# Products of row pairs on VectorE: per-row multiplies taken out, a larger share for ScalarE

## The chip, the cores and the metric

The kernel runs on one core of a Trainium2 chip. The metric is the device time of one execution in microseconds (us), from outside the kernel. A core has several engines with an instruction stream each. Three matter here: VectorE (DVE in the profile), ScalarE (ACT) and SyncE (SP), which here does nothing but issue DMA transfers. A transfer between the on-chip memory and HBM is split over 16 DMA engines, and it has landed when the last of them is done with its part.

## The reference

The input is a matrix of 4096 rows with 256 fp32 numbers each. For every row the kernel computes all products x[i]·x[j] with i ≤ j, in the order of the upper triangle: first the 256 products with i = 0, then 255 with i = 1, and so on to the single one with i = 255.

```python
dot = jnp.einsum('bi,bj->bij', inputs, inputs)
iu, ju = jnp.triu_indices(256)
return dot[:, iu, ju]          # (4096, 32896) fp32
```

The output has 4096 × 32896 × 4 bytes, 539 MB, from an input of 4.19 MB.

## The kernel before, in words

**Tiling.** The 4096 rows lie on 128 partitions, 32 rows to a partition. The whole input is loaded once into the tile x, by three DMAs (L124). Then the kernel walks over 16 groups (`g`); a group is REPEAT = 2 rows on every partition. In each group the 32896 output columns are cut into five pieces (`c`) of 6528 or 6592 columns. A piece of a group is one output tile o of 128 × 2 × 6592 numbers, 52 KB per partition, from a pool of three buffers (`opool`, bufs=3), and leaves by one DMA (L164). Only the very first piece leaves in four parts, cut at the columns in FIRST. So there are 16 × 5 + 3 = 83 output DMAs, all on SP's queue, in program order.

**Product rows.** A "product row" is a run of columns with one i: the number x[i] of a row times the stretch x[i..255] of the same row. `runs` lists the product rows of a piece as (i, j, at, n): first factor, first column of the second, place in the output, length n. Long rows come first: piece 0 has rows of 256 down to 231 products, piece 4 has rows of 114 down to 1. At a border of a piece a row is cut in two.

**Who computes what.** `split` gives the first (longest) product rows of a piece to ScalarE, as few as leave VectorE within a budget: BUDGET × REPEAT × columns, in nanoseconds by the kernel's own estimates (`vector_time`). ScalarE makes a product row with one ACTIVATE for each of the two repeats (L137), the number x[i] being the scale. With the budget of 1.08 ScalarE has no row of piece 0 in groups 1 to 15, and 2, 3, 4 and 15 rows of the pieces 1 to 4. In the very first piece the budget is 0: there the rows are halved between the engines by estimated time.

**VectorE's three ways.** `vector_ops` chooses among: "each", one tensor_scalar (L149) for each repeat of a row, x[i] as a per-partition scalar; "two", one tensor_tensor (L158) for two neighbouring rows and both repeats, where x[i] and x[i+1] are read with a step of 0; "all", one tensor_tensor for one row and both repeats. "Each" is chosen where the estimate REPEAT·(130 + 0.52·n) is not above that of the tensor_tensor. That is so for rows of some 215 products and more: all of piece 0, and about half of the columns of piece 1.

**Order.** `interleave` alternates between the first and the second half of a piece's operations, so that neighbouring instructions write far apart. Which engine waits for what is set by the framework: an engine's first instruction on a piece waits until the DMA that last emptied this buffer has landed; the DMA of a piece waits for both engines that wrote it.

Of the kernel before, what the change touches and what calls it, by code (L numbers as in the profile page):

```python
# [1 line left out]

# [4 lines left out]

F32 = mybir.dt.float32
AF = mybir.ActivationFunctionType
ALU = mybir.AluOpType  # L10

P = 128
UNIT = 64
REPEAT = 2
PIECES = 5
BUDGET = 1.08
FIRST = [512, 1536, 3584]


def even_borders(lo: int, hi: int, pieces: int) -> list[int]:  # L20
    units = (hi - lo) // UNIT
    return [lo + units * c // pieces * UNIT for c in range(pieces)] + [hi]


def runs(d: int, lo: int, hi: int) -> list:


    found, at = [], 0
    for i in range(d):
        a, b = max(at, lo), min(at + d - i, hi)  # L30
        if a < b:
            found.append((i, i + a - at, a, b - a))
        at += d - i
    return found


def vector_ops(block: list) -> list:

    ops, k = [], 0
    while k < len(block):
        i, j, at, n = block[k]
        two = k + 2 < len(block) and i == j
        each = REPEAT * (130 + 0.52 * n)
        together = 68 + 1.046 * REPEAT * n - (34 if two else 0)
        if each <= together:
            ops.append(("each", block[k]))  # L50
        elif two:
            ops.append(("two", block[k]))
            k += 1
        else:
            ops.append(("all", block[k]))
        k += 1
    return ops


def interleave(block: list) -> list:  # L60


    half = len(block)
    while half and len(vector_ops(block[:half])) > len(vector_ops(block[half:])):
        half -= 1
    a, b = vector_ops(block[:half]), vector_ops(block[half:])
    return [op for k in range(max(len(a), len(b))) for ops in (a, b) for op in ops[k : k + 1]]


def vector_time(block: list) -> float:  # L70
    t = 0.0
    for way, (i, j, at, n) in vector_ops(block):
        if way == "each":
            t += REPEAT * (130 + 0.52 * n)
        else:
            t += 68 + 1.046 * REPEAT * n * (2 if way == "two" else 1)
    return t


def split(block: list, budget: float) -> int:  # L80


    scalar, k = 0.0, 0
    while k < len(block):
        scalar += REPEAT * (184 + 0.837 * block[k][3])
        if vector_time(block[k:]) <= budget or scalar > vector_time(block[k + 1 :]):
            break
        k += 1
    return k


def window(ap: bass.AP, free: list) -> bass.AP:
    return bass.AP(ap.tensor, ap.offset, [list(ap.ap[0]), *free])


@with_exitstack
def kernel(
    ctx: ExitStack, tc: tile.TileContext, x: bass.AP, out: bass.AP
):

    nc = tc.nc
    n, d = x.shape
    width = out.shape[1]
    assert n % (P * REPEAT) == 0 and width == d * (d + 1) // 2 and width % UNIT == 0
    groups = n // (P * REPEAT)
    borders = even_borders(0, width, PIECES)
    slot = max(b - a for a, b in zip(borders, borders[1:]))  # L110

    xpool = ctx.enter_context(tc.tile_pool(name="x", bufs=1))
    opool = ctx.enter_context(tc.tile_pool(name="o", bufs=3))

    x_in = x.rearrange("(p r) d -> p (r d)", p=P)
    x_out = out.rearrange("(p g r) c -> g p r c", p=P, r=REPEAT)


    total = n // P * d
    xt = xpool.tile([P, total + 1], F32, name="x")  # L120
    nc.vector.memset(xt[:, total:], 0.0)  # L121
    cuts = [0, REPEAT * d, total // 2, total]
    for a, b in zip(cuts, cuts[1:]):
        nc.sync.dma_start(xt[:, a:b], x_in[:, a:b])  # L124

    for g in range(groups):
        for c, (lo, hi) in enumerate(zip(borders, borders[1:])):
            o = opool.tile([P, REPEAT, slot], F32, tag="o", name=f"o_{g}_{c}")
            first = g == c == 0
            cuts = [lo, *(FIRST if first else []), hi]  # L130
            for a, b in zip(cuts, cuts[1:]):
                block = runs(d, a, b)
                k = split(block, 0.0 if first else BUDGET * REPEAT * (b - a))
                for i, j, at, length in block[:k]:
                    for r in range(REPEAT):
                        row = (g * REPEAT + r) * d
                        nc.scalar.activation(  # L137
                            o[:, r, at - lo : at - lo + length],
                            xt[:, row + j : row + j + length],
                            AF.Copy,  # L140
                            scale=xt[:, row + i : row + i + 1],
                        )
                row = g * REPEAT * d
                for way, (i, j, at, length) in interleave(block[k:]):
                    at -= lo
                    if way == "each":
                        for r in range(REPEAT):
                            row_r = row + r * d
                            nc.vector.tensor_scalar(  # L149
                                o[:, r, at : at + length],  # L150
                                xt[:, row_r + j : row_r + j + length],
                                xt[:, row_r + i : row_r + i + 1],
                                None,
                                ALU.mult,
                            )
                        continue
                    m = 2 if way == "two" else 1
                    nc.vector.tensor_tensor(  # L158
                        o[:, :, at : at + m * length],
                        window(xt[:, row + j :], [[d, REPEAT], [1, m], [1, length]]),  # L160
                        window(xt[:, row + i :], [[d, REPEAT], [1, m], [0, length]]),
                        ALU.mult,
                    )
                nc.sync.dma_start(x_out[g][:, :, a:b], o[:, :, a - lo : b - lo])  # L164


# [1 line left out]
_INS = ["r_inputs"]  # L168
_OUTS = [((4096, 32896), "float32")]


# [20 lines left out]
```

## Time and profile before

| | before |
|---|---|
| time, median of 7 runs | 1277.84 us (1277.73 to 1278.0) |
| the profiled execution: its own time | 1277.79 us |
| span from first to last instruction in it | 1276.0 us |
| so outside the span | 1.79 us |
| VectorE busy | 1129.2 us, 2978 instructions |
| of these tensor_tensor (L158) | 805.7 us, 1651 |
| of these tensor_scalar (L149) | 346.1 us, 1326 |
| ScalarE busy | 234.7 us, 787 instructions |
| DMA over the span | 426 GB/s mean |

How to read it: busy time is the time in which an engine executed something, and idle time of an engine that is not the bottleneck costs nothing. The GB/s are what all 16 DMA engines moved together. The share of the DMA engines can be a little above 1 in short windows, since packets are counted whole.

### The profile page before, as it was taken

How to read it: one execution, taken by the hardware profiler on the slowest of the kernel's cores; microseconds unless marked ns; L12 is line 12 of the kernel's file. 1: busy time of each engine (PE TensorE's matmuls, PEld its weight loads, DVE VectorE, ACT ScalarE, POOL GpSimd, SP SyncE). 2: the span in 40 equal slices, each digit the busy share in tenths (PEclk: the TensorE clock that was granted, in tenths of full speed). 3: DMA queues.
4: the chain of work that ended last, by engine and by line, in shares of the span. 5: the costliest groups of instructions: out<-in, count | busy, mean ns of one | idle time of the engine just before them, and what ended most of it. 6: DMA issues, size and time to landing. Idle time of an engine off the chain costs nothing.

```text
span 1276.0 us, 4106 instructions
## 1 busy us (share of the span) xinstructions
DVE 1129.2 (88%) x2978; ACT 234.7 (18%) x787; POOL 0.2 (0%) x4
## 2 busy tenths in 40 slices
DVE  8999989898898988989889898898988989888880
ACT  4211112121121301213012130121301213012130
POOL 0000000000000000000000000000000000000000
DMA  9999999999999999999999999999999999999997
GB/s 387 431 435 428 430 431 426 433 424 434 430 430 429 430 431 426 435 423 434 425 433 429 429 434 425 433 425 434 428 430 432 427 433 425 433 425 434 428 430 314
DMA packets 23040, 543.43 MB, mean 426 GB/s; under 512 B 1376, under 2 KB 1376, under 8 KB 2016
## 3 DMA queue, kind: packets, MB, share of 16 engines
q1 hardware_dynamic: 23008, 543.17, 99.5%
q14 instruction: 32, 0.26, 0.0%
HBM read 4.19 MB, written 538.97 MB: 426 GB/s over the span
## 4 chain that ended last, share of the span: by engine, by line
DMA 62%; DVE 35%; issue 0%; DVEq 0%; SPq 0%
DMA out_dram<-o 62%; DVE o L158 24%; DVE o L149 11%; DMA x<-in_r_inputs_dram 0%; SPq L164 0%; DVEq L158 0%; DVEq L149 0%; DVEq L188 0%
## 5 line engine op out<-in xcount | busy, mean ns | idle before, releaser
L158 DVE TENSOR_TENSOR o<-x 128x104 f32<-128x104 f32 (+60 forms) x1651 | 805.7, 570 | 59.1 <-DMA out_dram<-o 59.1
L137 ACT ACTIVATE o<-x 128x197 f32<-128x197 f32 (+25 forms) x786 | 233.4, 384 | 1000.5 <-DMA out_dram<-o 918.8
L149 DVE TENSOR_SCALAR o<-x 128x216 f32<-128x216 f32 (+5 forms) x1326 | 346.1, 342 | 52.9 <-DMA out_dram<-o 50.2
L137 ACT ACT_TABLE_LOAD x1 | 1.3, 1283 | 0.7 <-PEq L179 0.7
L121 DVE MEMSET x<- 128x1 f32 x1 | 0.1, 59 | 0.8 <-PEq L179 0.8
L179 POOL MEMSET const-bfloat16-1.0<- 128x1 bf16 x1 | 0.1, 102 | 0.0
L179 POOL MEMSET const-uint8-127<- 128x1 uint8 x1 | 0.1, 101 | 0.0
L179 POOL MEMSET const-float32-0.0<- 128x1 f32 x1 | 0.1, 99 | 0.2 <-issue 0.2
L179 POOL MEMSET const-float32-1.0<- 128x1 f32 x1 | 0.1, 98 | 0.0
## 6 DMA issues: line engine op xcount, KB each, us to landing
out_dram<-o SPq DMA_DIRECT2D x64, 6592.0 KB, 32.9
out_dram<-o SPq DMA_DIRECT2D x15, 6528.0 KB, 33.3
out_dram<-o SPq DMA_DIRECT2D x1, 2944.0 KB, 16.7
x<-in_r_inputs_dram SPq DMA_DIRECT2D x1, 2048.0 KB, 12.5
out_dram<-o SPq DMA_DIRECT2D x1, 2048.0 KB, 13.7
x<-in_r_inputs_dram SPq DMA_DIRECT2D x1, 1792.0 KB, 7.1
out_dram<-o SPq DMA_DIRECT2D x1, 1024.0 KB, 11.7
out_dram<-o SPq DMA_DIRECT2D x1, 512.0 KB, 10.6
```

The source lines that it names most:

```text
L121: nc.vector.memset(xt[:, total:], 0.0)
L137: nc.scalar.activation(o[:, r, at - lo : at - lo + length], xt[:, row + j : row + j + length], AF.Copy, scale=xt[:, row + i : row + i + 1],)
L149: nc.vector.tensor_scalar(o[:, r, at : at + length], xt[:, row_r + j : row_r + j + length], xt[:, row_r + i : row_r + i + 1], None, ALU.mult,)
L158: nc.vector.tensor_tensor(o[:, :, at : at + m * length], window(xt[:, row + j :], [[d, REPEAT], [1, m], [1, length]]), window(xt[:, row + ...
L179: nc = _bacc.Bacc("TRN2", target_bir_lowering=False, num_devices=1)
```

## The change

VectorE loses the way "each": it makes pairs of rows by one tensor_tensor, and a row that has no partner by a tensor_tensor of its own. The budget goes from 1.08 to 0.95, so that `split` gives ScalarE more of the first rows of each piece. Loads, pieces, buffers, output DMAs and the order of the pieces stay.

```diff
-BUDGET = 1.08
+BUDGET = 0.95
...
     ops, k = [], 0
     while k < len(block):
         i, j, at, n = block[k]
-        two = k + 2 < len(block) and i == j
-        each = REPEAT * (130 + 0.52 * n)
-        together = 68 + 1.046 * REPEAT * n - (34 if two else 0)
-        if each <= together:
-            ops.append(("each", block[k]))
-        elif two:
-            ops.append(("two", block[k]))
-            k += 1
-        else:
-            ops.append(("all", block[k]))
-        k += 1
+        m = 2 if k + 2 < len(block) and i == j else 1
+        ops.append((block[k], m))
+        k += m
     return ops
...
 def vector_time(block: list) -> float:
-    t = 0.0
-    for way, (i, j, at, n) in vector_ops(block):
-        if way == "each":
-            t += REPEAT * (130 + 0.52 * n)
-        else:
-            t += 68 + 1.046 * REPEAT * n * (2 if way == "two" else 1)
-    return t
+    return sum(68 + 1.046 * REPEAT * n * m for (*_, n), m in vector_ops(block))
...
-                for way, (i, j, at, length) in interleave(block[k:]):
+                for (i, j, at, length), m in interleave(block[k:]):
                     at -= lo
-                    if way == "each":
-                        for r in range(REPEAT):
-                            row_r = row + r * d
-                            nc.vector.tensor_scalar(
-                                o[:, r, at : at + length],
-                                xt[:, row_r + j : row_r + j + length],
-                                xt[:, row_r + i : row_r + i + 1],
-                                None,
-                                ALU.mult,
-                            )
-                        continue
-                    m = 2 if way == "two" else 1
                     nc.vector.tensor_tensor(
```

What that makes of the two streams, counted in the instruction order of the built programs (an ACTIVATE on ScalarE is one row of one repeat):

| piece, groups 1 to 15 | ScalarE rows before → after | VectorE instructions before → after |
|---|---|---|
| 0 | 0 → 4 | 54 → 13 |
| 1 | 2 → 6 | 38 → 14 |
| 2 | 3 → 7 | 19 → 17 |
| 3 | 4 → 9 | 24 → 21 |
| 4 | 15 → 22 | 52 → 48 |

In the very first piece ScalarE keeps its nine rows, and VectorE's 39 instructions become 17. Over the whole program VectorE goes from 2978 to 1813 instructions and ScalarE from 787 to 1547, without those that only wait.

## The prediction

> **What bounds the kernel now.** I read the page first: busy shares, DMA slices, queues, issues.
>
> ```profile
> span 1276.0 us, 4106 instructions
> ...
> DVE 1129.2 (88%) x2978; ACT 234.7 (18%) x787; POOL 0.2 (0%) x4
> ...
> DMA  9999999999999999999999999999999999999997
> ...
> q1 hardware_dynamic: 23008, 543.17, 99.5%
> q14 instruction: 32, 0.26, 0.0%
> ...
> out_dram<-o SPq DMA_DIRECT2D x64, 6592.0 KB, 32.9
> ```
>
> The DMA engines are full in every slice but the last. A piece lands 32.9 us after its issue, and 6592 KB (6.75 MB) at the 430 GB/s of the middle slices take 15.7 us: two pieces are always queued, so VectorE, with 14.2 us of work in a piece, is early. The chain of waits gives it 35%, but only because the chain runs back through buffers; VectorE itself waits for landings (59.1 + 50.2 us). So the end is set by bytes. What is left is that a transfer ends with its *slowest* DMA engine. I looked at the busy time in windows at the end, when the last piece drains (columns: window, length, busy DVE, ACT, POOL, clock, DMA share, GB/s).
>
> ```profile
> 1266.00:1267.00 1.00, 0.00 (x0) 0.00 (x0) 0.00 (x0) 1.00 0.98 422
> 1267.00:1268.00 1.00, 0.00 (x0) 0.00 (x0) 0.00 (x0) 1.00 0.25 106
> 1268.00:1269.00 1.00, 0.00 (x0) 0.00 (x0) 0.00 (x0) 1.00 0.12 53
> 1269.00:1270.00 1.00, 0.00 (x0) 0.00 (x0) 0.00 (x0) 1.00 0.06 26
> ...
> 1273.00:1274.00 1.00, 0.00 (x0) 0.00 (x0) 0.00 (x0) 1.00 0.06 26
> 1274.00:1275.00 1.00, 0.00 (x0) 0.00 (x0) 0.00 (x0) 1.00 0.00 0
> ```
>
> A share of 0.06 is one engine of sixteen, 0.12 two. Most engines end at about 1267.2, a second-last one at about 1269, and one works alone until 1274: **6.8 us in which one DMA engine decides.** What has it done that the others have not? The page's last DMA row names the only other traffic: 32 packets of "instruction", 128 of the program's 4106 instructions in each. In a window of 1 us (286 to 287) one such packet takes 1.9% of 16 engines, 0.30 us. VectorE's 2978 instructions are 2978/128 = 23.3 packets, times 0.30 us 7.0 us, against 6.8 on the last engine; ScalarE's 787 are 6.1 packets, 1.8 us, against 1.8 on the second-last. I conclude that each engine's instructions come over one DMA engine, which so falls behind. The landings agree. ScalarE or VectorE starts a piece when a buffer's transfer has landed:
>
> ```profile
> 566.20 2.00 ACT L137 ACTIVATE o<-x 128x75 f32<-128x75 f32 x6 [14.26 <-DMA out_dram<-o]
> 581.56 2.63 ACT L137 ACTIVATE o<-x 128x143 f32<-128x143 f32 x8 [13.36 <-issue]
> 597.16 8.24 ACT L137 ACTIVATE o<-x 128x37 f32<-128x37 f32 x30 [12.97 <-DMA out_dram<-o]
> ```
>
> ```profile
> 613.50 13.86 DVE L149 TENSOR_SCALAR o<-x 128x256 f32<-128x256 f32 x54 [2.00 <-DMA out_dram<-o]
> 629.09 3.52 DVE L149 TENSOR_SCALAR o<-x 128x228 f32<-128x228 f32 x14 [1.73 <-DMA out_dram<-o]
> ```
>
> The steps are 15.36, 15.60, 16.34, 15.59 us. An instruction packet lies in the third stretch and in none of the others; the next stretch with a long step, 629.09 to 645.41 (16.32 us), has one again.
>
> **The change part by part.**
>
> *Instructions.* VectorE has 1165 fewer (2978 to 1813): 9.1 packets. At 0.30 us each its DMA engine falls behind by 2.7 us less: 6.8 − 2.7 = 4.1 us behind the rest. ScalarE has 760 more (787 to 1547), 5.9 packets: 1.8 + 1.8 = 3.6 us behind, so VectorE's stays the last, by 0.5 us. Gain **2.7 us**. Bounds for a packet: nothing from below (if the late engine is late for another reason), and from above the 0.75 us by which a landing with a packet comes later than one without (16.3 against 15.5); 9.1 × 0.75 = 6.8 would close the whole gap. I take 0.30: the tail adds up all 23 packets (6.8/23.3 = 0.29), while a landing shows a packet's first effect, part of which is caught up (15.36 is shorter than 15.6).
>
> The Trainium skill speaks against any effect: "Runtime: NRT & Kernel Launch", section "Instruction fetch mechanics", has instructions refilled in 16 KiB blocks of 256 by a queue of the sequencer's own, at a cost that is mostly hidden. It is hidden from the engine, as the trace agrees; but 32 packets of 8 KB (0.26 MB) are what the page has, and the tail shows where they go. By the rule the sum would be 0 and the time 1277.8 us.
>
> *VectorE's work.* A tensor_scalar takes 350 ns at 128x256, the tensor_tensor of 128x856 1046 and that of 128x400 580 ns (rows by shape). Start to start it is less: the chain has 0.96 us for a 128x856 and 0.49 us for two tensor_scalars of 224. From 856 and 400 elements a tensor_tensor costs (1046 − 580)/456 = 1.02 ns per element, and about 0.08 us on top start to start. Piece 0 keeps 5510 of its 6528 columns (rows 256 to 253 go): 13 instructions, 2 × 5510 × 1.02 ns + 13 × 0.08 = 12.3 us, against 13.86 now. Pieces 1 to 4 come to 12.2, 12.3, 12.3 and 12.8 us alike (5424, 5344, 5189, 4371 columns and 14, 17, 21, 48 instructions), from 14.2 to 14.4 now. All are under the 15.7 us of a transfer, with 31 us in the queue: **0 us**. Without that cover, if VectorE bound, the 1.5 to 2 us of a piece times 80 would be 120 us or more; nothing of it counts here.
>
> *ScalarE's work.* 30 activations of piece 4 take 8.24 us (row at 597.16), 0.275 each; 44 make 12.1 us. In the other pieces 8 to 18 activations, at the 0.47 us of the 128x229 row, are at most 8.5 us, all under 15.7: **0 us**. If ScalarE bound, the transfers would start late by what exceeds 31 us; it is far from that. In piece 0 ScalarE now waits for the buffer's landing, and the DMA for ScalarE too. Queued behind that wait is only its work on later pieces, whose buffers come free later still; and 3.3 us of ScalarE end long before VectorE's 12.3.
>
> *The start.* The queue fills from the loads on, so late first work could open a gap. The fourth DMA of the first piece is issued when VectorE ends that piece, at 13.2 us (in the chain 30 tensor_scalars follow from 9.29 us on in 7.40 us, the first 16 of them this piece's). Its 17 tensor_tensors take 0.6 to 0.8 us longer (9 ScalarE rows unchanged). The parts land 10.6, 11.7, 13.7 and 16.7 us after issue, for 1.2 to 7.0 us of bytes each: over 8 us of queue lie ahead of every one. The tightest is piece 1, issued at 27.5 us, with 18.1 us to landing (the issues of 27 to 28 us) for 15.7 us of bytes: 2.4 us of margin. It gains: 0.7 us later start, 1.9 us less work. **0 us.**
>
> *The queue.* SP issues the same three loads and 83 outputs, with the same sizes, in the same order: 0 us.
>
> Sum against the profiled execution: 1277.79 − 2.7 = **1275.1 us**, of which 1.79 lie outside the span as before. The median, 1277.84, stands 0.05 above it.
>
> **The rivals.**
>
> *Nothing moves* (1277.8 us): the late engine is late for something else, or ScalarE's packets, up from 6 to 12, load the same engine and take back 1.8 of 2.7 (1276.9). For it: no view says which engine a packet uses. Against it: two products, 7.0 and 1.8 us, fit two tails, 6.8 and 1.8.
>
> *The whole gap closes* (1271.0): with packets further apart each delay is caught up, at 0.75 us for each of the 9.1. Against it: in 23 packets not more than 0.29 us each was left over, so little is open to be caught up.
>
> *ScalarE's extra traffic slows the output* (slower than before). 760 activations more are busy for some 250 us (233.4 us now; the rows above add up to some 475). Windows of piece 4 with ScalarE busy and after it:
>
> ```profile
> 754.80:763.00 8.20, 8.20 (x25) 8.20 (x30) 0.00 (x0) 1.00 0.98 419
> 763.00:771.00 8.00, 6.13 (x28) 0.04 (x1) 0.00 (x0) 1.00 0.99 422
> ...
> 912.50:920.60 8.10, 8.10 (x25) 8.10 (x30) 0.00 (x0) 1.00 1.00 427
> 920.60:928.60 8.00, 6.17 (x28) 0.08 (x1) 0.00 (x0) 1.00 1.00 425
> ```
>
> 419 and 427 against 422 and 425: no sign, to within 1%. At 1.1% over 250 us (2.7 us) the gain is gone; from 2.1% on (5.3 us) the kernel is measurably slower; 3% gives 1275.1 + 7.5 = 1282.6 us.
>
> **How the numbers follow.** Forecast 0.62, nothing moves 0.20, whole gap 0.10, slower 0.08. The forecast's own spread is ±1 us (one packet more or less, at up to 0.75 us, and the second-last engine 0.5 us behind). The range takes the forecast, nearly all of "nothing moves" and the upper half of the way to the whole gap: 1273.3 to 1278.1; the ends left out are 1271 and 1283. A measurement of this kernel tells about 0.2% from no change, 2.56 us, so the line is at 1275.28, and the forecast at 1275.1 stands just beyond it: some 0.6 of its 0.62 falls there. Faster 0.37 + 0.10 = 0.47; same 0.25 + 0.20 = 0.45; slower 0.08.
>
> **What would show it.** Right: some 29 instruction packets instead of 32 on the page; most DMA engines end within 1 us of 1267.2, and the single engine's tail is some 4 us instead of 6.8, with a second one close to it; landings of 16.3 us come less often; VectorE is busy for about 990 us, ScalarE for about 480, and both wait longer for landings. Wrong: a tail of 6.8 us or more with fewer instructions; GB/s of the middle slices below 425; SP waiting with an empty queue; a landing less than 31 us after its issue in the middle.

## The result, and the profile after

| | before | after |
|---|---|---|
| median | 1277.90 us (34 runs, 1277.73 to 1278.05) | 1274.63 us (14 runs, 1273.79 to 1274.93) |
| the profiled execution | 1277.79 us, span 1276.0 | 1274.85 us, span 1273.1 |

The ratio of after to before is 0.9974, 95% interval 0.9967 to 0.9980: faster by 0.26%, 3.3 us. The profiled executions differ by 2.94 us. The page of the changed kernel, the lines that answer to those shown of before:

```profile
span 1273.1 us, 3732 instructions
...
DVE 996.1 (78%) x1813; ACT 486.7 (38%) x1547; POOL 0.2 (0%) x4
...
q14 instruction: 29, 0.24, 0.0%
...
out_dram<-o SPq DMA_DIRECT2D x64, 6592.0 KB, 34.8
```

VectorE is busy for 133 us less and ScalarE for 252 us more, and neither shows in the time: the queue is as full as it was (34.8 us from issue to landing). What has changed is in the instruction row, 29 packets instead of 32, and in the way the last piece drains (the busy time in windows at the end, columns as before):

```profile
1265.00:1266.00 1.00, 0.00 (x0) 0.00 (x0) 0.00 (x0) 1.00 1.17 501
1266.00:1267.00 1.00, 0.00 (x0) 0.00 (x0) 0.00 (x0) 1.00 0.43 185
1267.00:1268.00 1.00, 0.00 (x0) 0.00 (x0) 0.00 (x0) 1.00 0.13 53
...
1269.00:1270.00 1.00, 0.00 (x0) 0.00 (x0) 0.00 (x0) 1.00 0.12 53
1270.00:1271.00 1.00, 0.00 (x0) 0.00 (x0) 0.00 (x0) 1.00 0.06 26
1271.00:1272.00 1.00, 0.00 (x0) 0.00 (x0) 0.00 (x0) 1.00 0.00 0
```

Two DMA engines (0.12) now work on for some 4 us, one of them a little longer. Before, one worked alone until 1274. The last engine is earlier by 3 us, and ScalarE's has come close behind it.

The trace also has the 16 landing marks of each transfer, one for each DMA engine. They size the tail better than windows of 1 us, so the table has for every run of this study how far the last and the second-last part of the last transfer land behind the median part, and when that median part lands, from the span's start. The instructions are those of the built programs.

| run | VectorE / ScalarE instructions | packets on the page | last / second part behind the median, us | median part lands | time, median us |
|---|---|---|---|---|---|
| before | 2980 / 789 | 32 | 7.50 / 2.76 | 1267.6 | 1277.90 |
| after | 1815 / 1549 | 29 | 4.81 / 3.92 | 1267.3 | 1274.63 |
| e1 | 2935 / 1549 | 38 | 10.00 / 4.06 | 1267.7 | 1280.57 |
| e2 (GpSimd 1128) | 1815 / 1549 | 38 | 4.53 / 4.01 | 1267.7 | 1274.96 |
| e3 | 2618 / 1519 | 35 | 6.05 / 3.72 | 1266.8 | 1275.60 |
| e4 | 2006 / 851 | 24 | 4.56 / 1.94 | 1268.2 | 1275.53 |
| e5 | 2921 / 1549 | 37 | 6.78 / 4.13 | 1267.5 | 1277.37 |
| e6 | 3393 / 1549 | 41 | 9.77 / 3.88 | 1267.6 | 1280.05 |
| e7 | 1078 / 875 | 17 | 2.27 / 1.80 | 1283.2 | 1288.43 |
| e8 | 1014 / 1415 | 22 | 3.36 / 2.73 | 1282.2 | 1288.32 |
| e9 | 3238 / 2089 | 45 | 13.25 / 11.86 | 1261.8 | 1278.07 |
| e10 | 1719 / 1835 | 30 | 2.96 / 2.79 | 1265.7 | 1271.45 |

Of the 2.94 us between the two profiled executions, 2.69 are the last part's lag (7.50 to 4.81), and 0.26 are the median part, which lands earlier.

Landing by landing the marks also show whose packets delay which part. An instruction packet comes when VectorE's stream (instructions that only wait counted) stands 49 to 76 instructions past a multiple of 128, or ScalarE's 54 to 82; one packet in each of the two runs is SyncE's. In the kernel before, from the fourth piece on, the lag of the last part rises at 23 landings, by 0.6 to 0.8 us, and falls at all others, by some 0.15 us; each of the 23 follows a VectorE packet. In the changed kernel there are 14 such landings, with 0.7 to 1.0 us. Where a ScalarE packet comes alone before the change (at 271, 650, 840 and 1044 us), the second-last part rises, by 0.6 to 0.8 us, and the last one falls.

### The profile page after: what moved, and what is told of

Its sections match the earlier page's. It is cut to its first block, busy times and chain, and to the rows that moved or that the text cites. A ratio compares the mean times of both kernels' runs of the same rounds, so it can differ in the third digit from the quotient of the medians.

```text
span 1273.1 us, 3732 instructions
## 1 busy us (share of the span) xinstructions
DVE 996.1 (78%) x1813; ACT 486.7 (38%) x1547; POOL 0.2 (0%) x4
## 4 chain that ended last, share of the span: by engine, by line
DMA 68%; DVE 29%; issue 0%; SPq 0%; DVEq 0%
DMA out_dram<-o 67%; DVE o L132 29%; DMA x<-in_r_inputs_dram 1%; DVEq L132 0%; SPq L138 0%; SPq L110 0%
## 5 line engine op out<-in xcount | busy, mean ns | idle before, releaser
L132 DVE TENSOR_TENSOR o<-x 128x356 f32<-128x356 f32 (+61 forms) x1812 | 996.1, 634 | 240.3 <-DMA out_dram<-o 237.3
L123 ACT ACTIVATE o<-x 128x253 f32<-128x253 f32 (+41 forms) x1546 | 485.4, 404 | 749.1 <-DMA out_dram<-o 747.5
## 6 DMA issues: line engine op xcount, KB each, us to landing
out_dram<-o SPq DMA_DIRECT2D x64, 6592.0 KB, 34.8
x<-in_r_inputs_dram SPq DMA_DIRECT2D x1, 2048.0 KB, 12.2
```

Of the source, the lines that this page charges most:

```text
L123: nc.scalar.activation(o[:, r, at - lo : at - lo + length], xt[:, row + j : row + j + length], AF.Copy, scale=xt[:, row + i : row + i + 1],)
L132: nc.vector.tensor_tensor(o[:, :, at : at + m * length], window(xt[:, row + j :], [[d, REPEAT], [1, m], [1, length]]), window(xt[:, row + ...
```

## The experiments

The theory: the DMA engines set the time by bytes, and the end by the one among them that also carries VectorE's instruction packets; it loses some 0.30 us on each packet of 128 instructions. The rivals: the form of the work (tensor_scalars, or VectorE's busy time) slows the output; ScalarE's larger share helps; all instruction packets count, whichever engine they are for.

**e1: more VectorE instructions, nothing else.**

```diff
+    small = xpool.tile([P, 14], F32, name="small")
...
                 nc.sync.dma_start(x_out[g][:, :, a:b], o[:, :, a - lo : b - lo])
+            for k in range(14):
+                nc.vector.memset(small[:, k : k + 1], 0.0)
```

> The changed kernel, with 14 memsets of one column of a scratch tile added on VectorE behind each piece: 1120 instructions more (1815 to 2935), some 1 us of VectorE work in a piece that has 3 us to spare; nothing else reads the scratch tile. Theory (the end is set by the DMA engine that carries VectorE's instruction packets): 1120/128 = 8.75 packets at 0.30 us, +2.6 us, 1277.2 us; the lone tail of the last DMA engine grows from 4.8 to some 7.4 us. Rival, the form of work (tensor_scalars or VectorE's busy time slow the output, few instructions do not matter): no change, 1274.6 us, the same tail.

Measured: 1280.57 us, ratio to before 1.0020 (1.0011 to 1.0030). The rival of the form of work is out: instructions of 59 ns whose results nothing reads cost 5.9 us over the changed kernel. But that is more than twice the 2.6 us expected. The line's own instructions in the trace tell why; nothing tied the memsets to their piece, and they ran early:

```profile
L141 DVE MEMSET small<- x1120: 59/59/59, 0.8 to 178.8; 128x1 f32 x187
```

All 1120 ran in the first 179 us, and some nine packets came within eight pieces. At the end one DMA engine works alone for 6 us, after three together for 4:

```profile
1267.00:1271.00 4.00, 0.00 (x0) 0.00 (x0) 0.00 (x0) 1.00 0.19 79
1271.00:1277.00 6.00, 0.00 (x0) 0.00 (x0) 0.00 (x0) 1.00 0.06 26
1277.00:1278.00 1.00, 0.00 (x0) 0.00 (x0) 0.00 (x0) 1.00 0.00 0
```

The landing marks show how: at the tenth piece the last part was already 8.4 us late, at the twelfth 8.1, and 45 pieces further on 8.2. A packet first costs its DMA engine 0.6 to 1.0 us at the next landing; over the following pieces the engine makes up some 0.15 us in each, mostly until some 0.3 us are left. Packets that come faster than that pile up. But the 0.3 us are no constant: in those 45 pieces of e1 eight more VectorE packets came, and on balance they added nothing. Why is open.

**e2: the same instructions on GpSimd.**

```diff
-                nc.vector.memset(small[:, k : k + 1], 0.0)
+                nc.gpsimd.memset(small[:, k : k + 1], 0.0)
```

> The changed kernel, with the same 14 memsets per piece on GpSimd, which has no other work (8 to 1128 instructions). Theory: 8.75 packets more, but on a DMA engine of their own, which then lags by some 2.6 us, less than the 4.8 us of VectorE's: no change, 1274.6 us; three engines are late at the end instead of two. Rival, every instruction packet counts wherever it lands (traffic in all): +2.6 us, 1277.2 us, as with VectorE.

Measured: 1274.96 us, ratio 0.9977 (0.9968 to 0.9986). The page has 38 instruction packets, as in e1, and the time is 0.33 us above that of the changed kernel, with the last part no later (4.53 us) and the median part 0.38 us later. At the end:

```profile
1267.00:1270.00 3.00, 0.00 (x0) 0.00 (x0) 0.00 (x0) 1.00 0.25 105
1270.00:1271.00 1.00, 0.00 (x0) 0.00 (x0) 0.00 (x0) 1.00 0.12 53
1271.00:1272.00 1.00, 0.00 (x0) 0.00 (x0) 0.00 (x0) 1.00 0.00 0
```

Four DMA engines are late (0.25) where there were two, and none later than VectorE's; three were expected, and the fourth is taken up in the last section. So packets in all do not count; VectorE's, ScalarE's and GpSimd's each come over a DMA engine of their own, and the latest decides. GpSimd's nine packets came in the first 47 us and had put one part 4.9 us behind at the second piece; that part then stood at 2.8 us from the middle of the run to the end, 0.31 us for a packet: what a packet cost for good here.

**e5: the same instructions on VectorE, spread.**

```diff
                 row = g * REPEAT * d
+                if not first:
+                    start = block[k][2] - lo
+                    for q in range(14):
+                        nc.vector.memset(o[:, 0, start + q : start + q + 1], 0.0)
```

> As e1, but the 14 memsets of a piece write columns of the piece's own output tile, ahead of the products that overwrite them, so that they can't run early: 2921 VectorE instructions (2933 in e1, 1815 in the changed kernel), 14 more in each piece instead of all 1120 in the first 180 us. Theory (each packet costs its DMA engine 0.30 us for good, and some 0.5 us more that are made up over the next pieces unless the next packet comes first): +8.6 packets at 0.30, +2.6 us, 1277.2 us. Rival, VectorE instructions of this kind cost what e1 showed, wherever they stand: 1280.6 us.

Measured: 1277.37 us, ratio 0.9995 (0.9986 to 1.0004): +2.7 us on the changed kernel, and within 0.2 us of the forecast. In the profiled executions the lag of the last part accounts for 1.97 us of it, 0.23 us for a packet, where 2.6 were forecast. The same instruction count, spread, costs less than half of what it cost in e1; the lone engine ends 3 us earlier:

```profile
1270.00:1271.00 1.00, 0.00 (x0) 0.00 (x0) 0.00 (x0) 1.00 0.12 53
1271.00:1274.00 3.00, 0.00 (x0) 0.00 (x0) 0.00 (x0) 1.00 0.06 26
1274.00:1275.00 1.00, 0.00 (x0) 0.00 (x0) 0.00 (x0) 1.00 0.00 0
```

**e6: no pairs.** `interleave` puts each product row of VectorE in a tensor_tensor of its own; the share of ScalarE stays.

```diff
+def singles(block: list) -> list:
+    return [(row, 1) for row in block]
...
-    a, b = vector_ops(block[:half]), vector_ops(block[half:])
+    a, b = singles(block[:half]), singles(block[half:])
```

> The changed kernel with the same rows on each engine, but every product row of VectorE as a tensor_tensor of its own instead of pairs: 3393 VectorE instructions (1815), no tensor_scalar, some 1.4 us more VectorE work in a piece that has 3 us to spare. Theory: 1578 more are 12.3 packets, +3.7 us: 1278.3 us, slower than the kernel before, and up to 1280 if the packets, one in 2.9 pieces, come too close for the delays to be made up. Rival, what costs is the tensor_scalar form: 1274.6 us.

Measured: 1280.05 us, ratio 1.0017 (1.0008 to 1.0025). Without one tensor_scalar it is slower than the kernel before, and at the upper end of what was expected. The last part is 9.77 us late: its lag rises at 26 landings, by some 0.65 us each, and only 0.15 us are made up at each of the landings between, so packets that come closer leave more, 0.36 us each here.

**e3 and e4: the change in halves.** e3 is the kernel before with the budget of 0.95, e4 the changed kernel with 1.08.

```diff
-BUDGET = 1.08
+BUDGET = 0.95
...
-BUDGET = 0.95
+BUDGET = 1.08
```

> The kernel before with the budget of 0.95 alone; the tensor_scalars stay. VectorE has 2618 instructions (2980 before, 1815 after), ScalarE 1519 (789, 1549). Theory: 362 fewer on VectorE are 2.8 packets, -0.85 us: 1277.0 us. Rival, ScalarE's larger share (a lighter VectorE) is what helps: nearly the whole gain, 1274.6 us. Rival, the tensor_scalars are what costs: a part that goes with their number.

> The changed kernel with the old budget of 1.08: pairs alone, no tensor_scalars. VectorE has 2006 instructions (2980 before, 1815 after), ScalarE 851 (789, 1549). Theory: 974 fewer on VectorE are 7.6 packets, -2.3 us: 1275.6 us; ScalarE's DMA engine lags as before the change. Rival, the budget does it: 1277.9 us. Rival, the tensor_scalars are what costs: the whole gain, 1274.6 us.

Measured: e3 1275.60 us (ratio 0.9982, 0.9973 to 0.9991), e4 1275.53 us (0.9981, 0.9973 to 0.9990). e4's time is as forecast, but by two deviations that cancel: the lag of the last part fell by 2.94 us where 2.3 were expected, and the median part lands 0.64 us later than before. ScalarE stayed nearly as it was, so its share is not needed for most of the gain. e3 missed: 2.3 us gained where 0.85 were expected. The marks split it. The last part lags 6.05 us instead of 7.50: three packets fewer (0.9), and no VectorE packet in the last 70 us of the span, where before had one some 42 us ahead of the end whose first effect was not yet made up (two pieces' worth, some 0.3); some 0.2 us of it stay open. Another 0.75 us come from the other 15 engines: their median part lands at 1266.8 instead of 1267.6. In the early windows e3, here above the kernel before, moves more:

```profile
100.00:150.00 50.00, 40.18 (x116) 20.26 (x68) 0.00 (x0) 1.00 1.01 435
```

```profile
100.00:150.00 50.00, 49.79 (x130) 10.88 (x38) 0.00 (x0) 1.00 1.01 430
```

The theory has no term for that. The marks say where it arises. From 217 us on the median part needs the same 1050.3 to 1050.5 us in all eight runs with five pieces (before, after, e1 to e6). e3 gains its 0.8 us between 107 and 217 us, where its full transfers take some 15.6 us each and those of the kernel before 15.7; e4 loses its 0.6 us ahead of 107 us. It goes neither with instruction counts nor with ScalarE's share (the changed kernel and e2 have that share, and 1267.3 and 1267.7). Its cause is left open; it moves a run by up to 0.75 us.

**e7 and e8: fewer instructions by longer ones.** Four rows of a partition in a piece, ten pieces of half the columns; e7 (e8 keeps the budget of 0.95):

```diff
-REPEAT = 2
-PIECES = 5
-BUDGET = 0.95
-FIRST = [512, 1536, 3584]
+REPEAT = 4
+PIECES = 10
+BUDGET = 1.05
+FIRST = [512, 1536]
```

> A version to beat both: the changed kernel with four rows per partition in a piece instead of two, ten pieces of half the columns (same bytes per piece and buffer), first cuts at 512 and 1536, budget 1.05. A tensor_tensor covers four repeats, so VectorE has 1078 instructions (1815) and ScalarE 875 (1549). Theory: 5.8 packets fewer on VectorE's DMA engine, its lag goes from 4.8 to 3.1 us, ScalarE's to about 2: 1272.9 us. Rival: the transfers' runs are half as long (13 KB instead of 26 KB), which costs more than it gains: 1276 us or more.

> As e7 with the budget of 0.95: VectorE 1014 instructions, ScalarE 1415, so that ScalarE's DMA engine is the last. Theory: ScalarE's lag is that of the changed kernel less one packet, 3.6 us, VectorE's 2.9: 1273.4 us, 0.5 us above e7 although VectorE has fewer instructions. Rival, only VectorE's instructions count: as e7 or 0.1 us less.

Measured: 1288.43 and 1288.32 us, ratios 1.0082 (1.0068 to 1.0096) and 1.0081 (1.0067 to 1.0095). The times missed their forecasts of 1272.9 and 1273.4 us. The tails are short, 2.27 and 3.36 us where 3.1 and 3.6 were expected, the shortest of the study with three buffers; but the rival for e7 won. Mid-run windows of e7 and, below, of the kernel before:

```profile
200.00:300.00 100.00, 84.02 (x105) 23.35 (x84) 0.00 (x0) 1.00 1.01 424
600.00:700.00 100.00, 83.36 (x84) 21.67 (x75) 0.00 (x0) 1.00 1.01 424
```

```profile
200.00:300.00 100.00, 89.03 (x252) 22.42 (x78) 0.00 (x0) 1.00 1.00 430
600.00:700.00 100.00, 90.45 (x264) 19.57 (x68) 0.00 (x0) 1.00 1.00 429
```

With runs of 13 KB the DMA engines are as busy and move 1.3% less. The packets show it one by one: 13312 bytes take 504.6 ns on average in e7, 26368 bytes 984.7 ns before the change, 1.5% less for a byte. That is 16 us on e7's median part, against 2.5 us off its tail. Between e7 and e8 the tail differs by 1.1 us in the expected direction, the median part by as much the other way, and the times not at all, so "ScalarE's engine can be the last" stands on the tail alone.

**e9 and e10: longer runs.** The opposite way: e9 has one row in a piece and three pieces (44 KB runs), e10 four pieces (33 KB runs) with two buffers. The edits of e9, then those of e10:

```diff
-REPEAT = 2
-PIECES = 5
-BUDGET = 0.95
+REPEAT = 1
+PIECES = 3
+BUDGET = 0.90
```

```diff
-PIECES = 5
-BUDGET = 0.95
+PIECES = 4
+BUDGET = 0.85
...
-    opool = ctx.enter_context(tc.tile_pool(name="o", bufs=3))
+    opool = ctx.enter_context(tc.tile_pool(name="o", bufs=2))
```

> Another version to beat both, the other way round from e7: the changed kernel with one row per partition in a piece, three pieces (runs of 44 KB instead of 26), budget 0.90. e7 moved 424.5 GB/s in the middle with runs of 13 KB, the kernel before 430 with 26 KB; if the loss goes with the number of packets, 44 KB give 432.2 GB/s and 6.5 us less. VectorE has 3238 instructions (1815), ScalarE 2089 (1549): theory +11.1 packets, +3.3 us, up to +5 as in e6 where they come too close: 1271.4 to 1273.1 us, with the longest lone tail but e6. Rival, instructions do not matter at all in this one: 1268.1 us. Rival, longer runs bring nothing: 1278 us or more.

> Longer runs without more instructions: the changed kernel with four pieces of 33 KB runs, and two buffers instead of three, since three do not fit; budget 0.85. VectorE 1719 instructions (1815), ScalarE 1835 (1549). Theory: 33 KB give 431.1 GB/s and 3.2 us less; VectorE's lag falls by 0.2 us, ScalarE's rises by 0.7 to about the same: 1271.3 us. Rival, with two buffers the queue runs dry: a piece has 19.5 us of transfer, against 14 us of VectorE, some 2 us to start a transfer and 4.8 us of lag, so that the other DMA engines wait in each piece; if the late one waits too, by 1 us in each of 64 pieces, 1335 us.

Measured: e9 1278.07 us (1.0001, 0.9992 to 1.0010), e10 **1271.45 us** (0.9949, 0.9936 to 0.9963), the fastest of the study: 6.5 us under before, 3.2 under the changed kernel, 0.15 from its forecast. The split is not the forecast's, though: 3.2 us were expected from the longer runs and 0.2 from the tail, and the median part lands 1.6 us earlier than in the changed kernel while the last part's lag is 1.85 us smaller. A transfer there lands some 24.5 us after its issue, 19.5 of them its own:

```profile
out_dram<-o SPq DMA_DIRECT2D x32, 8256.0 KB, 24.5
out_dram<-o SPq DMA_DIRECT2D x31, 8192.0 KB, 24.9
```

So the queue is short, and still the latest DMA engine always has work; if the others run out of it now and then, it costs nothing at the end. The marks agree: from 873 us on every fourth transfer takes the median part 0.2 to 0.5 us longer, 2.0 us in all, and the lag of the last part shrinks there by about as much. That moves the split and leaves the sum.

e9 missed its forecast of 1271.4 to 1273.1 us. It gained from its runs most of what was expected (median part 5.5 us earlier than in the changed kernel, of 6.5) and lost more than expected in the tail (the last part's lag 8.4 us larger, where 3.3 to 5 were expected):

```profile
1262.00:1266.00 4.00, 0.00 (x0) 0.00 (x0) 0.00 (x0) 1.00 0.15 66
1266.00:1270.00 4.00, 0.00 (x0) 0.00 (x0) 0.00 (x0) 1.00 0.15 66
1270.00:1273.00 3.00, 0.00 (x0) 0.00 (x0) 0.00 (x0) 1.00 0.07 29
```

Its last part is 13.25 us late, by 26 VectorE packets: 0.5 us for a packet. Of a first delay of some 0.7 us only some 0.07 us is made up at a landing there, half of what it is with 26 KB runs. Why the making up depends on the runs is open. The second-last part, 11.86 us late, is not ScalarE's: it grows by some 0.25 us at every third transfer, with a packet or without (see the last section). ScalarE's 17 packets show in the third, 4.68 us late, 0.28 us for a packet.

## Why the prediction was right, point by point

- *The bound.* "The end is set by bytes", and then by the slowest DMA engine: right. VectorE's busy time fell by 12% and nothing followed from it; e1, e5 and e6 moved the time up with instructions alone, and e2 showed that the same number on GpSimd moves it by 0.33 us only.
- *Instructions.* 9.1 packets of VectorE fewer at 0.30 us, 2.7 us: the lag of the last part fell by 2.69 us. The row has 29 packets; the prediction said some 29. That the size agrees to 0.01 us is luck: the same price missed the last part's lag by some 0.6 us in e3, e4 and e5. The tails read from windows of 1 us, 6.8 and 1.8 us, were too small; the marks have 7.50 and 2.76. For ScalarE's engine 3.6 us behind the rest were forecast and 3.92 measured, which is near by two errors: it started 1.0 us higher, and its packets added 1.16 us instead of 1.8. It stays second, with 0.9 us to spare instead of 0.5. The choice of 0.30 between 0 and 0.75 was right for the packets here, one in 5.5 pieces. e1, e6 and e9 show that it is no constant: nearer packets cost up to 0.7 us, and in one stretch of e1 they added nothing.
- *The landings.* "Landings of 16.3 us come less often": VectorE's starts in the changed kernel, each at a landing:

```profile
107.95 12.38 DVE L132 TENSOR_TENSOR o<-x 128x612 f32<-128x612 f32 x21 [3.02 <-DMA out_dram<-o]
124.33 12.73 DVE L132 TENSOR_TENSOR o<-x 128x372 f32<-128x372 f32 x48 [4.00 <-DMA out_dram<-o]
139.89 12.48 DVE L132 TENSOR_TENSOR o<-x 128x1008 f32<-128x1008 f32 x13 [2.83 <-DMA out_dram<-o]
155.46 12.38 DVE L132 TENSOR_TENSOR o<-x 128x896 f32<-128x896 f32 x14 [3.09 <-DMA out_dram<-o]
```

  The first stretch, 16.38 us, has an instruction packet. The second has one too, ScalarE's by its place in the stream, and takes 15.56: it fell on a DMA engine that is not the last.
- *VectorE's and ScalarE's work at 0 us.* Right, with the sizes: 12.4 to 12.7 us a piece in these rows (12.2 to 12.8 forecast), 11.97 us for the 44 activations (12.1), 996 and 487 us busy (990 and 480). VectorE waits some 3 us before each piece.
- *The start and the queue at 0 us.* Right; no gap opened, and the slices of the middle stand at 428 to 433 GB/s.
- *The rule of the Trainium skill, "Runtime: NRT & Kernel Launch", section "Instruction fetch mechanics"*, that refilling is mostly hidden, would have made it 1277.8 us. Hidden it is where the packets are not on the latest DMA engine (e2, +0.33 us with GpSimd's nine), and not where they are (e5, +2.74 us with about as many of VectorE's): the measurement decides against the rule here.
- *The rivals.* "Nothing moves" fell with the time and the last part's lag; "ScalarE's packets load the same engine" with the marks, where they raise another part than VectorE's; "the whole gap closes" with the 4.81 us left; "ScalarE's traffic slows the output" with the GB/s above.
- *What the sum did not have.* 2.7 us were forecast and 2.94 measured against the profiled execution, 3.27 between the medians. The rest, 0.26 us, is the other 15 DMA engines' earlier landing, which e3 and e4 show to move by 0.6 to 0.75 us for a reason that is not settled; and the changed kernel's runs lie 1.1 us apart where before they lie 0.3 apart, so a single execution says less about it.

## What to carry to other kernels

When the DMA engines are full and the computing engines wait, look at the last microseconds of the drain: a share of 1/16 there is one DMA engine alone, and what delayed it here was worth more than 133 us of VectorE's busy time. The instruction streams of VectorE, ScalarE and GpSimd were each traffic on one of these DMA engines, in most runs some 0.3 us for 128 instructions if they were spread and up to 0.7 if they were not, so fewer and longer instructions on the engine with the most of them helped although that engine waits in each piece. Weigh that against the length of a transfer's runs: 13 KB instead of 26 KB cost six times what fewer instructions gave (e7).

## What was not expected of the hardware

- A packet's first delay, 0.6 to 1.0 us at the next landing for 0.31 us of transfer, is made up at some 0.15 us a landing with runs of 26 KB, and at some 0.07 us with 44 KB.
- With many instructions one more DMA engine is late (4.06 us in e1, 3.22 in e2, 3.16 in e5, 2.78 in e3, 11.86 in e9). It is the one that SyncE's single packet delays, by 0.5 to 0.6 us at some 540 us in e1 and e2 and at 436 us in e9; the rest of its lag comes without packets, evenly through e3, e5 and e9, and while the memsets ran in e1 and e2. The number of instructions alone does not give it: e6 has more than any other run with five pieces, and 2.18 us. It never decides, and what delays it is open.
- Two buffers instead of three show no cost in e10, whose forecast had none, although the queue then holds little more than one transfer.
